# A graph network kernel on one core: one more group of columns copied by VectorE, and the hand-made jobs begun earlier

## The chip, the cores and the metric

The kernel runs on one core of one Trainium2 chip. The metric is the device time in microseconds. The engines are named as in the profile: PE is TensorE (PEld its weight loads), DVE is VectorE, ACT is ScalarE, POOL is GpSimd and SP is SyncE, which here only issues DMAs.

## The reference, cut to what matters

```python
h = relu(layernorm(x))                              # x: 12500 nodes x 128
m = relu(concat(h[src], h[dst], edge_attr) @ w1 + b1) @ w2 + b2   # 400000 edges, sorted by dst
agg = segment_sum(m, dst)
out = x + gru(agg, h)                               # gates r, z, n over w_ih, w_hh
```

The edges are sorted by their target node `dst`; their source nodes `src` are random. So a row per edge has to be fetched by `src`, 400,000 in all.

## The kernel before, in words

**Ahead of the loop.** The first stage normalises all nodes, keeps h transposed on the chip (`hT_all`, 128 features x 12500 nodes) and stores the table A = h @ w1[0:128] in HBM, so that an edge needs one row of A instead of a matmul. It also stores B, the part of the target nodes.

**Groups and units.** The edges form 3125 tiles of 128. Eight tiles make a group, 391 groups in all (the first has five tiles); a group is worked in two units of four tiles, units 0 to 781. Units -7 to -1 run ahead of the loop and hold only the steps that work ahead. In unit u the function `stages` (L1151) issues: the statistics of raw rows for unit u+7 (`raw_stats`, VectorE, and a root on ScalarE, L234), their end and the norms for u+6 (`raw_fin`, and `raw_h`, four norms on ScalarE, L292), the turning of the raw rows for u+4 (`raw_turn`: TensorE L699, copied by VectorE L701), the matmuls of u+3 (`pre`, L716), the one-hot tables (L615, L666), and the add of the fetched rows for u+2 (`add`, VectorE, once for a whole group in its second unit; L748). Behind it `seg` (L774) sums the edges of unit u into their nodes. Every engine takes its instructions in this order.

**Where the rows of a group come from.** Four ways:

- Groups 0 to 8 (`RAW`) are fetched by GpSimd from x, since A is not there yet; they need statistics, norms, turning and a relu on ScalarE (L760).
- Most groups are fetched by GpSimd from A, one indirect DMA for a tile (`gather`, L158, issued at L170). The fetched rows lie in 11 buffers G that go round (`GBUFS`, `ring`, L149). So a gather for the group at place j of this ring waits until the group at place j-11 has let go of its buffer: a raw group at its turning, another at its add.
- 30 groups go to VectorE and 29 to ScalarE as **column jobs**: a gather of 1024 columns of `hT_all` on the chip, four bytes on each partition at a time, by an address in a register. ScalarE copies them one by one (`one_by_one`, L1062, register loads of 16 at L1049); VectorE takes two columns in one instruction (`Pairs`, L1021, register loads of 32), and untangles 64 pairs by a byte copy (L1032). TensorE then multiplies with w1 (L727), and the add becomes a plain relu on VectorE (L743).
- 5 groups go to SyncE as **row jobs**: 1024 row DMAs from A.

**Who gets which group, and when.** `SPREAD` (L57) has the counts and `START` (L58) the unit at which each engine's first job begins. The loop at L92 spreads the groups evenly between START//2+2 and a fixed distance from the end. A job runs from the end of the one before (or START) to a few units before its group is needed: 2k-4 for ScalarE, 2k-6 for VectorE, 2k-8 for SyncE. ScalarE's and SyncE's jobs are cut into four phases of a unit (`run_jobs`, L1118): phase 0 ahead of `stages`, the others behind it. VectorE's pairs go by the due numbers of `pairs_due` (L1069), put around long instructions by `before_long`, `some` and `behind_long`. Before the change ScalarE's first groups are 17, 30, 43 and VectorE's 21, 34, 46; the last are 388 and 386.

**The places.** The source numbers of the groups in jobs are brought as rows of a table `at` (`at_row`, L448, DMAs on SyncE's queue in the first stage). One VectorE instruction (L1209) scales them to addresses (`place_of` holds factor and offset for each row). Row 64 of `at` is used by another step, so that a 65th job gets row 65 (`row_of`), and two small fills make row 64 whole.

Of the kernel before, what the change touches and what calls it, by code (L numbers as in the profile page):

```python
# [17 lines left out]
ALU = mybir.AluOpType  # L18
# [35 lines left out]
STEP = {"act": 4, "sp": 4}  # L54
QUEUE = 10
ROW = 4 * D
SPREAD = {"dve": 30, "act": 29, "sp": 5}  # L57
START = {"dve": 14, "act": 4, "sp": 24}  # L58
NR = 12672

H_AT = 16512
# [3 lines left out]
def tile_gnn(ctx: ExitStack, tc: tile.TileContext, x, src, srcT, dstT, dstP, eaT, eaP, w1, b1, w2T, b2,  # L65
             wih, bih, whh, bhh, out):
    nc = tc.nc
# [23 lines left out]

    mode, order = {}, {m: [] for m in SPREAD}  # L92
    for m, n in SPREAD.items():
        lo, hi = START[m] // 2 + 2, NP - {"dve": 5, "act": 3, "sp": 12}[m]
        for i in range(n):
# [34 lines left out]
    at = const.tile([128, PAIR * 128], I32, name="at")  # L130
# [71 lines left out]
    def row_of(k):  # L202
        r = by_hand.index(k)
        return r if r < 64 else r + 1

    ROWS = row_of(by_hand[-1]) + 1
# [3 lines left out]
    place_of = const.tile([ROWS, 2], F32, name="place_of")  # L210
# [397 lines left out]
    def onehot_T(k):  # L608
        if k >= NP:
            return  # L610
        c = slice((k % QP) * 512, (k % QP + 1) * 512)
        o, i = Ls[k // QP][:2 * V, c], Ls[k // QP].bitcast(I32)[:2 * V, c]
        n = k - BLOCKS[-1][0]
        if n < 0:
            nc.vector.tensor_scalar(o, i, node_of[:, k:k + 1], None, op0=ALU.is_equal)  # L615
        else:
            nc.vector.tensor_scalar(o, i, node_of[:, k:k + 1], 0.0, op0=ALU.is_equal, op1=ALU.add,
                                    accum_out=dlast[:2 * V, n:n + 1])
# [58 lines left out]
    def raw_h(u):  # L677
        if u < 2 * RAW:
            for i, s in enumerate(slots(u)):
                relu_norm(unit(u)[:, s, :], unit(u)[:, s, :], HE[u][:, i, :])  # L680

    def raw_stats(u):
        if u < 2 * RAW:
            l = slots(u)
            HE[u] = bn_sqrt(p2, bn(p2, lambda j: unit(u)[:, l[j], :], 128, len(l)), 128, len(l))

    def raw_fin(u):
        if u < 2 * RAW:
            n = len(slots(u))
            st = p2.tile([128, GRP, 2], F32, name="st_raw", bufs=4)  # L690
            bn_fin(p2, st[:, :n, :], HE[u], 128, n)
            HE[u] = st

    def raw_turn(u):
        if u < 2 * RAW:
            l = slots(u)
            pt = ps1.tile([128, 512], F32, name="misc")
            for i, s in enumerate(l):
                nc.tensor.transpose(pt[:, i * 128:(i + 1) * 128], unit(u)[:, s, :], ident)  # L699
            hT = p3.tile([128, 512], F32, name="gt", bufs=3)  # L700
            nc.vector.tensor_copy(hT[:, :len(l) * 128], pt[:, :len(l) * 128])  # L701
            HE[u] = hT
# [54 lines left out]
    def relu(u):  # L757
        if u in RT:
            o, p = RT.pop(u)
            nc.scalar.activation(o, p, AF.Relu)  # L760
# [276 lines left out]
    def one_by_one(m, k):  # L1037
        et = {"act": ET.Activation, "sp": ET.SP}[m]
        r = row_of(k)
        if m == "sp":  # L1040
            goal[k] = tc.alloc_semaphore(f"brought{r}"), 16 * PAIR * 128
            G[k] = pj.tile([128, GRP, 2, D], F32, name="G_sp", bufs=1)
            rows = G[k].bitcast(U8)
        else:
            hand[k] = pj.tile([128, PAIR * 128], F32, name=f"HE_{m}")
            he = hand[k].bitcast(U8)
        for e0 in range(0, PAIR * 128, LOAD[m]):
            low, high = (0, ROW * (N - 1)) if m == "sp" else (H_AT, H_AT + 4 * (N - 1))
            _, vals = nc.values_load_multi_w_load_instructions(  # L1049
                at[r:r + 1, e0:e0 + LOAD[m]], engines=[et], min_val=low, max_val=high,  # L1050
                skip_runtime_bounds_check_because="src holds numbers of nodes")
            for i, v in enumerate(vals):
                e = e0 + i
                if m == "sp":
                    a, j = divmod(e // 128, GRP)
                    fetched = put(rows[e % 128:e % 128 + 1, j, a, :],
                                                A_bytes[bass.ds(v, ROW)].rearrange("(o f) -> o f", o=1))
                    fetched.then_inc(goal[k][0], 16)
                    tc.no_tile_sem_insts.add(fetched.ins.name)
                    tc.add_to_no_dep_group(f"rows{k}", fetched.ins)  # L1060
                else:
                    nc.scalar.copy(he[:, e * 4:e * 4 + 4], column(v))  # L1062
                if i % STEP[m] == STEP[m] - 1:
                    yield
# [4 lines left out]
    def pairs_due():  # L1069
        start, n = START["dve"], 0  # L1070
        for k in order["dve"]:
            end = 2 * k - 6
            for u in range(start, end):
                due[u] = n + -(-(PAIR * 64 * (u + 1 - start)) // (end - start))
            n += PAIR * 64
            start = end
# [3 lines left out]
    def behind(u):  # L1080
        return due.get(u, cols.end if u >= START["dve"] else 0) - cols.done

# [4 lines left out]
    def before_long(u, ops):  # L1087
        if u == START["dve"]:
            cols.load()
        some(u, cols.end, QUEUE - ops)  # L1090
        if cols.turn and u % 2 == 0:
            some(u, cols.end, QUEUE - ops - 1)
            cols.part()

    def behind_long(u, least):
        if behind(u) >= least:
            cols.pairs(cols.left())
            cols.load()
# [9 lines left out]
    for m in ("act", "sp"):  # L1108
        start = START[m]
        for k in order[m]:  # L1110
# [5 lines left out]
    PH = 4  # L1116

    def run_jobs(u, phase):  # L1118
        if phase == 0:
            for m, k, span in jobs.get(u, ()):  # L1120
                live[m] = [one_by_one(m, k), u, span, PAIR * 128 // STEP[m], 0]
        for m, job in list(live.items()):
            it, start, span, steps, done = job
            want = -(-steps * ((u - start) * PH + phase + 1) // (span * PH))
            while job[4] < want:
                job[4] += 1
                if next(it, "end") == "end":
                    del live[m]
                    break
# [4 lines left out]
    def gathers(u):  # L1134
        while asked[0] < NP and (asked[0] in mode or 2 * taker[asked[0]] + 1 < u + 2):
            gather(asked[0])
            asked[0] += 1
# [13 lines left out]
    def stages(u):  # L1151
        if u + 7 >= 0:
            raw_stats(u + 7)
        if u + 6 >= 0:
            raw_fin(u + 6)
            raw_h(u + 6)
        if u + 4 >= 0:
            raw_turn(u + 4)
        if u + 3 >= 0:
            pre(u + 3)  # L1160
        before_long(u, 2 if u % 4 == 2 else 1)
        if u % 2 == 0:
            onehot_T(u // 2 + 3)
            onehot(u // 2 + 3)
        if u + 2 >= 0:
            add(u + 2)
            relu(u + 2)
        behind_long(u, 1)

    for u in range(-7, 0):  # L1170
        stages(u)
    nodes_left = []

    def step(left):
# [13 lines left out]
    for u in range(NU):  # L1188
        k, h = divmod(u, 2)
        gathers(u)  # L1190
        if h == 0:
            window_rows(k + 4)
            if k % QP == 1:
                fetch(k // QP + 3)
            if k and k == BLOCKS[block(k)][0]:
                nodes_left.append([node(block(k) - 1), 2 if k < BLOCKS[-1][0] else 1])
            if k % PLACE == 1:
                indices(k // PLACE + 2)
            if k % PLACE == 5:
                place(k // PLACE + 1)  # L1200
                dst_tile(k // PLACE + 2)
            if k == 6:
                late_setup()
            if k == 20:
                store_stats()
            if k == NP - 20:
                check_windows()
        if u == min(START.values()) - 2:
            nc.vector.tensor_scalar(at[:ROWS, :], at[:ROWS, :], place_of[:, 0:1], place_of[:, 1:2],  # L1209
                                    op0=ALU.mult, op1=ALU.add)  # L1210

        run_jobs(u, 0)
        stages(u)
        run_jobs(u, 1)
        some(u, 4, QUEUE - 1)
        run_jobs(u, 2)
        some(u, 4, QUEUE - 1)
        seg(u)
        if u == 0:
            node_setup()  # L1220
        run_jobs(u, 3)
        some(u, cols.end, QUEUE - 1)
        worked[0] = False
        if h == 0:
            take(k - 1)
        step(nodes_left)
        if u in LAST_STEPS:
            next(last)
        behind_long(u, 4 if worked[0] else 14)
        in_time(u)  # L1230
# [173 lines left out]
```

## Time and profile before

| what | before |
|---|---|
| median of 3 runs | 3344.64 us (3341.72 to 3346.97) |
| the profiled execution | 3339.77 us, span 3338.0 us |
| TensorE's mean granted clock in it | 0.807 |
| gathers of GpSimd (L170) | 69 from x, 2544 from A |
| column copies of ScalarE (L1062) | 29696 |
| column pairs of VectorE (L1021) | 15360 |
| row DMAs of SyncE into G_sp | 5120 |

How to read it: the span is from the first to the last instruction, and the 1.8 us beside it lie around them. A row of a group shows the line, the engine, the operation, output and input, the count; then busy time and the mean duration of one in ns; then the engine's idle time just ahead of these instructions and what ended most of it. "issue" stands for idle time in which nothing that the profile shows was waited for. A row of the timeline shows the start in us, the duration in us, the instruction, and in brackets the idle time ahead of it with what ended it. A duration includes the pipeline's ends, so instructions of one engine overlap a little; the pitch of a series is taken from start to start.

### The profile page before, as it was taken

To read this page: it belongs to the slowest core of one execution; us is meant where nothing else is said; L and a number is where in the kernel's file an instruction comes from. 1 tells how busy PE (TensorE), PEld (TensorE's weight loads), DVE (VectorE), ACT (ScalarE), POOL (GpSimd) and SP (SyncE) were. 2 spreads that over 40 slices of the span, in tenths; PEclk is the share of its full clock that TensorE was granted. 3 is DMA by queue.
4 is the path that set the end of the run, shared out by engine and by line. 5 is a ranking of instruction groups with operands and counts; after the bars stand their busy time and mean duration, and the time that the engine had idled before them with its cause. 6 is when DMAs were issued, how large, how long until landed. Compare 5 with 4: busy or idle time off the path is not lost. (4 is left out here: it accounts for less than half of the span.)

```text
span 3338.0 us, 96341 instructions
## 1 busy us (share of the span) xinstructions
PE 2404.0 (72%) x13177; PEld 1556.9 (47%) x13177; DVE 2391.7 (72%) x17889; ACT 3133.3 (94%) x30026; POOL 2515.3 (75%) x2622
## 2 busy tenths in 40 slices
PE   7567777777777777767776777676677677767767
PEld 6444444444454445444444444454344444444445
DVE  8567777777777777777767777776676777676765
ACT  6599999999999999999999989998989999899985
POOL 7777777777777777777777777777777777777775
PEclk9878878888877787878777878778787788777878
DMA  6433443444344444444343444443443444444332
GB/s 213 107 88 89 99 101 98 100 95 106 96 101 94 102 95 99 104 102 97 95 100 98 99 99 100 98 100 89 98 99 93 101 95 99 95 97 99 93 95 72
DMA packets 195740, 333.85 MB, mean 100 GB/s; under 512 B 68936, under 2 KB 117639, under 8 KB 195095
## 3 DMA queue, kind: packets, MB, share of 16 engines
q0 software_dynamic: 83616, 171.41, 22.6%
q1 hardware_dynamic: 111335, 156.20, 17.3%
q14 instruction: 536, 4.39, 0.4%
q8 instruction: 109, 1.79, 0.2%
q10 hardware_dynamic: 144, 0.07, 0.0%
HBM read 307.17 MB, written 20.24 MB: 98 GB/s over the span
## 5 line engine op out<-in xcount | busy, mean ns | idle before, releaser
L1062 ACT COPY HE_act<-hT_all 128x4 uint8 x29696 | 2990.7, 189 | 52.5 <-issue 27.5
L170 POOL DMA_INDIRECT G<-A,src_i x2544 | 2448.5, 962 | 782.4 <-issue 748.0
L1021 DVE SCALAR_TENSOR_TENSOR both<-hT_all 128x4 uint16 x15360 | 1314.9, 153 | 673.3 <-issue 635.7
L716 PE MATMUL pre<-RW,L 128*128 128x256 f32 x3128 | 1113.4, 481 | 10.4 <-DMA RW<-B 10.4
L774 PE MATMUL seg<-RB,OH 128*32 128x129 f32 x6250 | 610.5, 327 | 668.7 <-DVE RB L748 577.4
L774 PEld LDWEIGHTS seg<-RB,OH 128*32 128x32 f32 x6250 | 335.2, 126 | 981.3 <-DVE RB L748 659.4
L716 PEld LDWEIGHTS pre<-RW,L 128*128 128x128 f32 x3128 | 653.5, 233 | 286.5 <-issue 212.9
L748 DVE CUSTOM_DVE_ANT_0 RB<-pre,G 128x1024 f32<-128x1024 f32 x319 | 386.0, 1210 | 83.8 <-DMA G<-A,src_i 76.6
L615 DVE TENSOR_SCALAR L<-L,node_of 64x512 f32<-64x512 int32 x382 | 188.5, 493 | 51.8 <-DMA L<-in_dstP 51.6
L666 DVE TENSOR_TENSOR OH<-dloc,seg 128x512 f32<-128x512 f16 (+1 forms) x198 | 131.1, 663 | 0.0
L801 PE MATMUL nd<-spot,sums 128*128 128x40 f32 x782 | 119.7, 325 | 9.4 <-DVE sums L783 9.4
L801 PEld LDWEIGHTS nd<-spot,sums 128*128 128x128 f32 x782 | 114.8, 235 | 18.7 <-DVE sums L783 10.2
L1032 DVE COPY HE_dve<-both 128x512 uint8<-128x512 uint8 x240 | 103.4, 431 | 0.0
L727 PEld LDWEIGHTS pre<-w1a,HE_act 128*128 128x128 f32 x464 | 87.4, 234 | 12.6 <-ACT HE_act L1062 1.8
L806 PE MATMUL misc<-spot_h,dcol 128*128 128x40 f16 x382 | 45.3, 194 | 66.5 <-DVE dcol L831 61.4
L727 PEld LDWEIGHTS pre<-w1a,HE_dve 128*128 128x128 f32 x480 | 84.8, 221 | 9.5
L727 PE MATMUL pre<-w1a,HE_act 128*128 128x128 f32 x464 | 85.9, 316 | 1.4 <-ACT HE_act L1062 1.4
L727 PE MATMUL pre<-w1a,HE_dve 128*128 128x128 f32 x480 | 83.8, 304 | 0.0
L170 POOL DMA_INDIRECT G<-in_x,src_i x69 | 65.4, 947 | 21.8 <-issue 20.7
L851 PE MATMUL nd<-DEG,brow 34*128 34x512 f32 (+2 forms) x112 | 65.6, 667 | 20.5 <-ACT gt L861 18.7
L743 DVE TENSOR_SCALAR RB<-pre 128x1024 f32<-128x1024 f32 x59 | 71.6, 1213 | 7.0 <-PE pre L727 6.9
L806 PEld LDWEIGHTS <-dcol 128*128 128x128 f16 x382 | 37.0, 105 | 81.0 <-DVE dcol L831 69.8
(178 smaller groups left out, 1357.0 us busy)
## 6 DMA issues: line engine op xcount, KB each, us to landing
G_sp<-A SPq DMA_DIRECT2D x5120, 0.5 KB
L<-in_dstP SPq DMA_DIRECT2D x195, 256.0 KB
L<-in_eaP SPq DMA_DIRECT2D x195, 256.0 KB
G<-A,src_i POOLq DMA_INDIRECT x2544, 3.3
RW<-B SPq DMA_DIRECT2D x782, 16.0 KB
xb<-in_x SPq DMA_DIRECT2D x26, 256.0 KB
out<-xb SPq DMA_DIRECT2D x26, 256.0 KB
xs<-in_x SPq DMA_DIRECT2D x11, 512.0 KB
```

The lines of the kernel that those rows point to most:

```text
L170: fetched = nc.gpsimd.indirect_dma_start(out=G[k][:, j, a, :], out_offset=None, in_=table, in_offset=bass.IndirectOffsetOnAxis(ap=src_i[c] ...
L615: nc.vector.tensor_scalar(o, i, node_of[:, k:k + 1], None, op0=ALU.is_equal)
L666: nc.vector.tensor_tensor(p, dloc[:, e0:e1, None].to_broadcast(shape), row[:, None, :].to_broadcast(shape), op=ALU.is_equal)
L716: nc.tensor.matmul(p[:, 2 * i:2 * i + 2, :], Ls[k // QP][:, c0:c0 + 128], RW[k % 4], start=True, stop=not raw)
L727: nc.tensor.matmul(p[:, 2 * i + a, :], cols, w1a, start=False, stop=n + 1 == len(l) or l[n + 1][1] != j)
L748: made = nc.vector._custom_dve(TENSOR_ADD_SAT, out=o, in0=p, in1=G[k].rearrange("p j a f -> p (j a) f")[:, c, :], s0=float("inf"), s1=0.0)
L774: nc.tensor.matmul(p[r0:r0 + V, :D + 1], OH[k][:, a * GRP + j, :], RB[k % 2][:, 2 * j + a, :D + 1], start=False, stop=all(b != a for _, _, ...
L801: nc.tensor.matmul(p[:, bass.ds(offs[i], V + SHIFT)], sums[:, slot(b, i), :D], spot[:, i % 2, :], start=False, stop=i == len(offs) - 1)
L806: nc.tensor.matmul(p[:, bass.ds(offs[i], V + SHIFT)], t[:, c:c + 128], spot_h[:, a, :], start=False, stop=i == len(offs) - 1)
L1021: nc.vector.scalar_tensor_tensor(self.both[:, e % PIECE // 2, :], column(second), 256.0, column(first), op0=ALU.mult, op1=ALU.add)
L1032: nc.vector.tensor_copy(hand[k].bitcast(U8)[:, p0 * 4:(p0 + PIECE) * 4].rearrange("p (n c b) -> p n c b", c=2, b=4), both.bitcast(U8).rear ...
L1062: nc.scalar.copy(he[:, e * 4:e * 4 + 4], column(v))
```

## The change

VectorE gets 31 groups instead of 30. The first jobs begin at unit 8 for VectorE (14 before), -6 for ScalarE (4 before) and 8 for SyncE (24 before), and the groups are spread anew from these starts: ScalarE's first groups are now 12, 25, 39, VectorE's 18, 30, 42; the last are 388 and 386 as before. The scaling of the places moves from unit 2 of the loop to a place ahead of unit -7, and the units ahead of the loop call `run_jobs` as the loop does. With 65 jobs the table `at` has 66 rows. The groups that GpSimd fetches go from 327 to 326.

```diff
-SPREAD = {"dve": 30, "act": 29, "sp": 5}
-START = {"dve": 14, "act": 4, "sp": 24}
+SPREAD = {"dve": 31, "act": 29, "sp": 5}
+START = {"dve": 8, "act": -6, "sp": 8}
...
+    nc.vector.tensor_scalar(at[:ROWS, :], at[:ROWS, :], place_of[:, 0:1], place_of[:, 1:2],
+                            op0=ALU.mult, op1=ALU.add)
     for u in range(-7, 0):
+        run_jobs(u, 0)
         stages(u)
+        for phase in range(1, PH):
+            run_jobs(u, phase)
...
-        if u == min(START.values()) - 2:
-            nc.vector.tensor_scalar(at[:ROWS, :], at[:ROWS, :], place_of[:, 0:1], place_of[:, 1:2],
-                                    op0=ALU.mult, op1=ALU.add)
-
         run_jobs(u, 0)
         stages(u)
```

## The prediction

> **What bounds the kernel now.** I read the page's first and fifth parts, then GpSimd's waits and its timeline.
>
> ```profile
> PE 2404.0 (72%) x13177; PEld 1556.9 (47%) x13177; DVE 2391.7 (72%) x17889; ACT 3133.3 (94%) x30026; POOL 2515.3 (75%) x2622
> L1062 ACT COPY HE_act<-hT_all 128x4 uint8 x29696 | 2990.7, 189 | 52.5 <-issue 27.5
> L170 POOL DMA_INDIRECT G<-A,src_i x2544 | 2448.5, 962 | 782.4 <-issue 748.0
> L1021 DVE SCALAR_TENSOR_TENSOR both<-hT_all 128x4 uint16 x15360 | 1314.9, 153 | 673.3 <-issue 635.7
> ```
>
> By busy share ScalarE (94%) looks like the bound and GpSimd (75%) does not. But GpSimd's 782.4 us of idle time are nearly all "issue": a fixed gap ahead of each gather. The waits of GpSimd, and four rows of its timeline:
>
> ```profile
> POOL G L170 <- issue: 768.8, 2521, 0.3
> POOL G L170 <- DVE RB L748: 5.9, 14, 1.9
> ```
> ```profile
> 124.75 0.94 POOL L170 DMA_INDIRECT G<-A,src_i  x1 [2.49 <-PE misc L699]
> 206.81 0.94 POOL L170 DMA_INDIRECT G<-A,src_i  x1 [1.91 <-DVE RB L748]
> 237.26 0.95 POOL L170 DMA_INDIRECT G<-A,src_i  x1 [0.30 <-issue]
> 3319.33 0.94 POOL L170 DMA_INDIRECT G<-A,src_i  x1 [0.30 <-DMA G<-A,src_i]
> ```
>
> A gather takes (2448.5+782.4)/2544 = 1.270 us from start to start, and they run back to back until 3320.3 us; the span ends at 3338. Nothing holds GpSimd after 206.81 us: there it waited 1.9 us for the add of group 9 (L748), which frees the buffer that group 22 needs. From then on GpSimd alone sets the end. Who reads its rows is behind it at first and catches up late:
>
> ```profile
> DVE both L1021 <- issue: 311.0, 394, 2.6
> DVE RB L748 <- DMA G<-A,src_i: 76.6, 31, 5.8
> ```
>
> This is VectorE's waiting from 1800 us to the end: 31 adds waited for rows, 76.6 us. So two things move the end: the number of gathers, one for one, and anything that delays GpSimd's restart at 206.81, also one for one, since that wait was already above the fixed gap.
>
> **What goes: eight gathers.** VectorE takes a 31st group, so 8 x 1.270 = 10.2 us leave GpSimd. The jobs that end last stay on groups 386 (VectorE) and 388 (ScalarE), so the 17.7 us behind the last gather stay. 10.2 is thus the most that this part can give.
>
> Against it stand eight more byte copies of VectorE (L1032). Two gathers beside such a copy:
>
> ```profile
> 242.67 0.41 DVE L1032 COPY HE_dve<-both 128x512 uint8<-128x512 uint8 x1
> 251.00 0.42 DVE L1032 COPY HE_dve<-both 128x512 uint8<-128x512 uint8 x1
> ```
> ```profile
> 242.26 0.95 POOL L170 DMA_INDIRECT G<-A,src_i  x1 [0.30 <-issue]
> 251.00 1.24 POOL L170 DMA_INDIRECT G<-A,src_i  x1 [0.30 <-issue]
> ```
>
> The copy that begins 0.4 us into a gather leaves it at 0.95; the one that begins with it lengthens it to 1.24. Bounds: 0 to 8 x 0.30 = 2.4 us. I take 0, since most gathers stand at 0.94 and the mean of 0.962 holds all lengthening there is. The Trainium skill (SBUF — State Buffer, section Who interferes with whom) says that a VectorE copy in a two-port mode and a GpSimd instruction lock each other out for a whole instruction, whichever issues first. By that rule eight copies of 0.42 would give back at most 3.4 us; the pair of rows agrees with its order of issue, not with a full block.
>
> **What moves: ScalarE's first job.** It used to begin in unit 4 and ends up in unit -6. Its 1024 copies go over 26 units either way (30-4, now 20+6), 39.4 a unit; ten units of them, 396 with the rounding to steps of four, come ahead of unit 4. Where ScalarE stands there now:
>
> ```profile
> 90.00:143.00 53.00, 25.63 (x151) 20.44 (x152) 29.73 (x168) 20.88 (x53) 36.73 (x39) 0.71 0.39 101
> 143.00:206.00 63.00, 39.95 (x271) 31.75 (x271) 34.81 (x203) 62.96 (x493) 46.97 (x50) 0.89 0.34 84
> ```
>
> From 90 to 143 it is busy 20.9 of 53 us; from 143 to 206 it is busy throughout (62.96 of 63). So an idle stretch of 32.1 us is offered 396 copies, and behind it no room is left. The copies' pitch and that of the work between, from ScalarE's timeline:
>
> ```profile
> 103.22 0.30 ACT L234 ACTIVATE s<-mv,eps 128x4 f32<-128x4 f32 x1 [10.58 <-DVE mv L229]
> 104.24 0.88 ACT L292 ACTIVATE G<-G,st_raw 128x128 f32<-128x128 f32 x2 [0.73 <-DVE st_raw L247]
> 124.77 0.30 ACT L234 ACTIVATE s<-mv,eps 128x4 f32<-128x4 f32 x1 [10.88 <-DVE mv L229]
> 142.95 1.23 ACT L1062 COPY HE_act<-hT_all 128x4 uint8 x12
> 145.82 4.04 ACT L1062 COPY HE_act<-hT_all 128x4 uint8 x40
> 149.76 0.29 ACT L234 ACTIVATE s<-mv,eps 128x4 f32<-128x4 f32 x1
> 149.96 1.63 ACT L292 ACTIVATE G<-G,st_raw 128x128 f32<-128x128 f32 x4
> 151.50 1.00 ACT L760 ACTIVATE RB<-pre 128x1024 f32<-128x1024 f32 x1
> 152.41 4.06 ACT L1062 COPY HE_act<-hT_all 128x4 uint8 x40
> ```
>
> Start to start, 40 copies take 3.94 us (98.5 ns each), a root 0.20, four norms 1.54, a relu 0.91. In program order 52 copies (unit -6 and the first phase of -5) stand ahead of the root at 103.22, which waits for VectorE, and fit into its 10.58 us; 5 us of that wait stay idle. The two norms at 104.24 end by 105.1. From there to unit 4: 344 copies x 0.0985 = 33.9, eight roots 1.6, eight times four norms 12.3, three relus 2.7, in all 50.5 us, so unit 4 begins at 155.6 instead of 142.95: **12.7 us late**. With the copies at the mean of their whole group, (2990.7+52.5)/29696 = 102.5 ns, it is 14.1. The later roots find their statistics ready: the one that waited until 124.77 is now reached at about 126 (105.1, 156 copies, three roots, twelve norms). I take 13.
>
> Is this lateness passed on? From 143 on ScalarE has no gap, and the order of its work in units 4 to 13 is what it was. The relu of group 6 lets TensorE turn the last raw rows, for which VectorE waits:
>
> ```profile
> 187.63 1.00 ACT L760 ACTIVATE RB<-pre 128x1024 f32<-128x1024 f32 x1
> ```
> ```profile
> 101.29 0.48 DVE L615 TENSOR_SCALAR L<-L,node_of 64x512 f32<-64x512 int32 x1 [9.95 <-DMA L<-in_dstP]
> 190.84 0.69 DVE L701 COPY gt<-misc 128x512 f32<-128x512 f32 x1 [3.45 <-PE misc L699]
> 193.39 0.73 DVE L1021 SCALAR_TENSOR_TENSOR both<-hT_all 128x4 uint16 x8 [1.85 <-issue]
> 205.33 1.21 DVE L748 CUSTOM_DVE_ANT_0 RB<-pre,G 128x1024 f32<-128x1024 f32 x1
> 239.66 1.21 DVE L748 CUSTOM_DVE_ANT_0 RB<-pre,G 128x1024 f32<-128x1024 f32 x1
> ```
>
> The chain is relu at 187.63, copy at 190.84 (3.45 us waited), VectorE's queue in order, the add of group 9 at 205.33, GpSimd at 206.81. No link has slack.
>
> **VectorE's column jobs** now begin in unit 8, not 14, at 512 pairs over 22 units (23.3 a unit) in both. A pair costs 1314.9/15360 = 86 ns, with the idle time behind register loads (1314.9+635.7)/15360 = 127 ns. In units 8 to 12 they mostly fill waits for ScalarE. In unit 13, behind the copy at 190.84, one unit of pairs is new: 2.0 to 3.0 us, less up to 1.85 us of first load that is over earlier. If VectorE falls behind already in units 8 to 12, I allow 2 us more. Bounds 0 to 5; I take 2.
>
> **A second wait of GpSimd.** With group 12 taken by ScalarE, the buffer needed three groups after group 22 is that of group 13, not 12. GpSimd was at 237.26 then; the add of group 13 ended at 239.66+1.21 = 240.9. Both shift alike, so GpSimd waits 3.6 us plus the 0.3 from an add's end to a gather: 3.9, bounds 3.6 to 4.7.
>
> **Taken at nothing.** The scaling (L1209), the row loads from HBM (L107) and ScalarE's register loads (L1049):
>
> ```profile
> L1209 DVE TENSOR_SCALAR at<-at,place_of x1: 876/876/876, 134.1 to 134.1; 64x1024 int32<-64x1024 int32 x1
> L107 SPq DMA_DIRECT2D at<-in_src x64: 238/254/839, 21.4 to 83.7; - x64
> L1049 ACTq TENSOR_LOAD <-at x1856: 1007/1045/2193, 140.6 to 3301.6; - x186
> ```
>
> The scaling moves from 134.1 to about 88, ahead of VectorE's 9.95 us wait at 101.29, which hides it; without that cover, 0.9. The 65th row is one more issue of 0.25 us on SyncE by 84, before the scaling; two small fills are paid early by VectorE, at most 0.5. SyncE's five jobs start 16 units sooner at the same rate, about seven row loads a unit (7 x 0.25 = 1.8 us of a 4 us unit): 0, at most 3 if they delay a load of L that VectorE then waits for.
>
> **Sum.** -10.2 + 13 + 2 + 3.9 = **+8.7 us**. Against the profiled execution (3339.77, span 3338.0) that is 3348.5; the median of the three runs is 4.9 higher, so I predict 3344.6 + 8.7 = **3353.3**. Its own bounds: 12.7 to 14.1, 0 to 5, 3.6 to 4.7, and 0 to 3 and 0 to 2.4 for the rest give +6.1 to +19, with most of it from +6 to +14.
>
> **Rivals.**
>
> Copies hidden by their loads (faster). Each 16 copies need a register load of 1.045 us in ScalarE's queue, while 16 copies take 1.576 at the pitch above. If the load is the price and runs on behind norms and waits, a copy costs (1.576-1.045)/16 = 33 ns, 344 of them 11.4 instead of 33.9, and unit 4 is not late at all. Then GpSimd restarts at 206.8 to 209 and waits again for 0 to 3.9: -10.2 to -4, 3334 to 3341. Against it: the 40 copies at 145.82 follow four norms directly and show no hidden load. It decides from the first copies ahead of the loop: a pitch under 60 ns.
>
> VectorE becomes the bound (slower still). 512 more pairs at 127 ns are 65 us; some 140 pairs are drawn ahead of the add of group 9, so 373 fall behind it, 47 us, against a spare of 76.6-10.2 = 66. At the mean duration and all idle time, 153 + 673.3/15360 = 197 ns a pair, it would be 73, and the reader ends 7 us after the rows: +16, 3361. For it speaks that both sides are of one size; against it, that 153 ns is a duration and not a pitch. It decides if the adds never wait for rows at the end.
>
> The early jobs do not start early. If the first load waits for hT_all or the places until 103 or later, the 52 copies lose their cover, 5 us more delay: +14, 3358. If they were held back as far as unit 4, the loop would begin on time and only the gathers and the second wait change: -6, 3338. The last row load is issued at 83.7, 4 us before the scaling's new place, which speaks against both.
>
> **Chances.** The forecast's mechanism 0.70, of which 0.17 small enough to lie within 0.2% (+6.7); copies hidden 0.15; VectorE as bound 0.10; not early 0.05. What a measurement of this kernel can tell from no change is about 0.2%, 6.7 us. With 0.13 of the hidden copies and 0.02 of the last case counted as faster, and 0.02 of the hidden copies as no change: faster 0.15, same 0.20, slower 0.65. The range 3341 to 3364 leaves out most of the hidden copies (0.13) and the far ends (0.05).
>
> **What would show it.** In the changed profile: 2605 gathers; ScalarE's copies from about 90 us; its first copy that belonged to unit 4 near 156; GpSimd held long before the first gather of group 22, near 222 instead of 206.81, and again three groups later by some 4 us; no hold after 350; the last gather near 3328, with the adds still waiting for rows after 2200 us. It is wrong if GpSimd passes 207 on time, or if its last gather has long been done when the reader arrives.

## The result, and the profile after

| what | before | after |
|---|---|---|
| median of 4 runs each | 3343.44 us (3341.72 to 3346.97) | 3362.49 us (3360.74 to 3364.20) |
| the profiled execution | 3339.77, span 3338.0 | 3360.74, span 3358.9 |
| gathers, first to last | 69 + 2544 | 69 + 2536 |

The change makes the kernel **slower**: the ratio is 1.0056, 95% interval 1.0038 to 1.0073, that is 12.7 to 24.4 us with 19 in the middle. Between the two profiled executions the spans differ by 20.9 us. The profiled execution is the fastest of its kernel each time, that of before by more (3.7 us below the median of 3343.44, that of after 1.7 below 3362.49), so that the spans differ by some 2 us more than the medians. The forecast was +8.7, its range reached to +19.4. The sign and the place are as forecast, the size is about twice it.

The first and fifth parts of the page of after. The columns are those of before.

```profile
PE 2379.5 (71%) x13193; PEld 1542.5 (46%) x13193; DVE 2430.6 (72%) x18411; ACT 3133.4 (93%) x30026; POOL 2513.5 (75%) x2614
L170 POOL DMA_INDIRECT G<-A,src_i x2536 | 2446.6, 965 | 805.4 <-issue 744.7
L1062 ACT COPY HE_act<-hT_all 128x4 uint8 x29696 | 2991.4, 189 | 55.9 <-issue 28.1
L1021 DVE SCALAR_TENSOR_TENSOR both<-hT_all 128x4 uint16 x15872 | 1355.0, 153 | 698.8 <-issue 663.9
```

The busy shares have hardly moved; from the page alone one could not say why the kernel is slower. The line to look at is GpSimd's: eight gathers less, and yet 23 us more of idle time ahead of them (805.4 against 782.4), 3.3 us less of it "issue". What ended the rest stands in GpSimd's waits (us in total, times, the longest), and its place in GpSimd's timeline:

```profile
POOL G L170 <- DVE RB L748: 20.5, 15, 12.0
POOL G L170 <- PE misc L699: 14.9, 6, 3.5
```
```profile
227.87 0.94 POOL L170 DMA_INDIRECT G<-A,src_i  x1 [12.05 <-DVE RB L748]
262.32 0.94 POOL L170 DMA_INDIRECT G<-A,src_i  x1 [4.50 <-DVE RB L748]
3340.62 0.94 POOL L170 DMA_INDIRECT G<-A,src_i  x1 [0.30 <-DMA G<-A,src_i]
```

GpSimd waits 20.5 us for adds instead of 5.9, 16.6 of them in two places: ahead of group 22 it is held until 227.87 instead of 206.81, and three groups of its ring later, until 262.32, where it had passed at 237.26 without a wait. Behind that no wait is longer than 0.6 us, up to the last gather, which ends at 3341.56. The second row, waits for TensorE, stands ahead of both: five of the six lie between 156.40 and 206.12, where GpSimd needs the buffers of raw groups, whose turning ScalarE's lateness now delays. They lie within the first stretch below, and do not add to it: group 22 goes when the add of group 9 is done, however early GpSimd stands there. From these rows and those of before the whole difference can be added up:

| stretch | before | after | more |
|---|---|---|---|
| start to the first gather of group 22 | 206.81 | 227.87 | +21.1 |
| from there to the second hold's end | 30.45 | 34.45 | +4.0 |
| from there to the end of the last gather | 3083.0, 2432 gathers of 1.2677 | 3079.2, 2424 of 1.2703 | -3.8 |
| behind it to the end of the span | 17.7 | 17.3 | -0.4 |
| span | 3338.0 | 3358.9 | +20.9 |

The third row is -10.1 for eight gathers and +6.4 for a pitch that is 2.6 ns longer over 2424 of them.

**Why group 22 is late.** ScalarE's timeline of after, and the row of before in which unit 4's root stands:

```profile
92.56 1.24 ACT L1062 COPY HE_act<-hT_all 128x4 uint8 x12 [1.10 <-DVE st_raw L245]
104.22 0.30 ACT L234 ACTIVATE s<-mv,eps 128x4 f32<-128x4 f32 x1 [5.13 <-DVE mv L229]
105.89 4.05 ACT L1062 COPY HE_act<-hT_all 128x4 uint8 x40
109.84 0.29 ACT L234 ACTIVATE s<-mv,eps 128x4 f32<-128x4 f32 x1
156.91 0.29 ACT L234 ACTIVATE s<-mv,eps 128x4 f32<-128x4 f32 x1
200.65 1.00 ACT L760 ACTIVATE RB<-pre 128x1024 f32<-128x1024 f32 x1
```
```profile
144.08 0.30 ACT L234 ACTIVATE s<-mv,eps 128x4 f32<-128x4 f32 x1
```

The copies begin at 92.56; 40 of them take 3.95 us (105.89 to 109.84), 98.7 ns each, the same pitch as in the loop. Unit 4's root comes 12.8 us late (156.91 against 144.08), and the relu of group 6 13.0 us late (200.65 against 187.63). The windows of before showed ScalarE 20.9 us busy from 90 to 143; after (us of PE, PEld, DVE, ACT and POOL in order):

```profile
90.00:143.00 53.00, 21.32 (x119) 16.77 (x120) 27.95 (x156) 45.28 (x348) 37.43 (x40) 0.70 0.40 105
```

It is 24.4 us more busy, and 7.7 us stay idle. Most of this is one wait, 5.1 us for VectorE ahead of the root at 104.22: only 52 copies stand before that root in ScalarE's order, and the next must wait behind it. VectorE adds to this. Its copies of the turned raw rows (L701) are one to a unit, so they can be laid side by side. First those of before, with the waits for ScalarE between them, then those of after:

```profile
162.86 0.68 DVE L701 COPY gt<-misc 128x512 f32<-128x512 f32 x1
168.63 0.18 DVE L240 RECIPROCAL y<-s 128x4 f32<-128x4 f32 x1 [3.44 <-ACT s L234]
169.57 0.68 DVE L701 COPY gt<-misc 128x512 f32<-128x512 f32 x1
174.23 0.18 DVE L240 RECIPROCAL y<-s 128x4 f32<-128x4 f32 x1 [1.83 <-ACT s L234]
175.16 0.68 DVE L701 COPY gt<-misc 128x512 f32<-128x512 f32 x1
180.81 0.18 DVE L240 RECIPROCAL y<-s 128x4 f32<-128x4 f32 x1 [3.97 <-ACT s L234]
181.78 0.68 DVE L701 COPY gt<-misc 128x512 f32<-128x512 f32 x1
186.12 0.68 DVE L701 COPY gt<-misc 128x512 f32<-128x512 f32 x1
```
```profile
176.29 0.68 DVE L701 COPY gt<-misc 128x512 f32<-128x512 f32 x1
184.23 0.68 DVE L701 COPY gt<-misc 128x512 f32<-128x512 f32 x1
190.02 0.68 DVE L701 COPY gt<-misc 128x512 f32<-128x512 f32 x1
195.24 0.18 DVE L240 RECIPROCAL y<-s 128x4 f32<-128x4 f32 x1 [1.40 <-ACT G L292]
196.18 0.68 DVE L701 COPY gt<-misc 128x512 f32<-128x512 f32 x1
203.49 0.68 DVE L701 COPY gt<-misc 128x512 f32<-128x512 f32 x1
208.55 0.69 DVE L701 COPY gt<-misc 128x512 f32<-128x512 f32 x1 [1.24 <-issue]
226.38 1.22 DVE L748 CUSTOM_DVE_ANT_0 RB<-pre,G 128x1024 f32<-128x1024 f32 x1
```

Subtract each row of before from its partner (the waits are those for ScalarE and TensorE; idle time behind register loads, "issue", is not counted as one):

| from copy to copy | pairs before, after | VectorE's wait there before | took before, after | lateness at its end |
|---|---|---|---|---|
| (at 162.86 / 176.29) | | | | 13.4 |
| to 169.57 / 184.23 | 0, 23 | 3.44 | 6.71, 7.94 | 14.7 |
| to 175.16 / 190.02 | 0, 16 | 1.83 | 5.59, 5.79 | 14.9 |
| to 181.78 / 196.18 | 0, 25 | 3.97 | 6.62, 6.16 | 14.4 |
| to 186.12 / 203.49 | 0, 23 | none | 4.34, 7.31 | 17.4 |
| to 190.84 / 208.55 | 0, 25 | 3.45 | 4.72, 5.06 | 17.7 |
| to the add of group 9, 205.33 / 226.38 | 71, 103 | none | 14.49, 17.83 | 21.05 |

ScalarE's 13 us are there before the first early pair is drawn. Where VectorE used to wait, the pairs cost 1.2, 0.2, -0.5 and 0.3 us; in the two stretches without a wait they cost 3.0 and 3.3. Together 7.6 us. Behind 195.24 VectorE no longer waits for ScalarE at all on the way to the add of group 9. This split goes by the order of time; it does not say what each early start would cost without the other.

### The profile page after: what moved, and what is told of

It is laid out like the page before. It is cut to its first block, busy times and chain, and to the rows that moved or that the text cites. A ratio compares the mean times of both kernels' runs of the same rounds, so it can differ in the third digit from the quotient of the medians.

```text
span 3358.9 us, 96915 instructions
## 1 busy us (share of the span) xinstructions
PE 2379.5 (71%) x13193; PEld 1542.5 (46%) x13193; DVE 2430.6 (72%) x18411; ACT 3133.4 (93%) x30026; POOL 2513.5 (75%) x2614
## 3 DMA queue, kind: packets, MB, share of 16 engines
q1 hardware_dynamic: 111337, 156.20, 17.3%
## 5 line engine op out<-in xcount | busy, mean ns | idle before, releaser
L170 POOL DMA_INDIRECT G<-A,src_i x2536 | 2446.6, 965 | 805.4 <-issue 744.7
L1021 DVE SCALAR_TENSOR_TENSOR both<-hT_all 128x4 uint16 x15872 | 1355.0, 153 | 698.8 <-issue 663.9
L748 DVE CUSTOM_DVE_ANT_0 RB<-pre,G 128x1024 f32<-128x1024 f32 x318 | 384.7, 1210 | 74.7 <-DMA G<-A,src_i 73.4
L615 DVE TENSOR_SCALAR L<-L,node_of 64x512 f32<-64x512 int32 x382 | 185.6, 486 | 13.6 <-DMA L<-in_dstP 13.6
L666 DVE TENSOR_TENSOR OH<-dloc,seg 128x512 f32<-128x512 f16 (+1 forms) x198 | 131.1, 662 | 0.0
L801 PE MATMUL nd<-spot,sums 128*128 128x40 f32 x782 | 104.2, 299 | 13.8 <-DVE sums L783 13.8
L801 PEld LDWEIGHTS nd<-spot,sums 128*128 128x128 f32 x782 | 99.3, 207 | 22.0 <-DVE sums L783 14.6
L1032 DVE COPY HE_dve<-both 128x512 uint8<-128x512 uint8 x248 | 108.0, 436 | 0.2 <-issue 0.2
L727 PEld LDWEIGHTS pre<-w1a,HE_act 128*128 128x128 f32 x464 | 80.5, 217 | 9.1
L170 POOL DMA_INDIRECT G<-in_x,src_i x69 | 65.5, 950 | 21.9 <-issue 20.7
L743 DVE TENSOR_SCALAR RB<-pre 128x1024 f32<-128x1024 f32 x60 | 72.8, 1214 | 5.2 <-PE pre L727 5.2
```

The lines of the kernel that those rows point to most:

```text
L170: fetched = nc.gpsimd.indirect_dma_start(out=G[k][:, j, a, :], out_offset=None, in_=table, in_offset=bass.IndirectOffsetOnAxis(ap=src_i[c] ...
L666: nc.vector.tensor_tensor(p, dloc[:, e0:e1, None].to_broadcast(shape), row[:, None, :].to_broadcast(shape), op=ALU.is_equal)
L727: nc.tensor.matmul(p[:, 2 * i + a, :], cols, w1a, start=False, stop=n + 1 == len(l) or l[n + 1][1] != j)
L748: made = nc.vector._custom_dve(TENSOR_ADD_SAT, out=o, in0=p, in1=G[k].rearrange("p j a f -> p (j a) f")[:, c, :], s0=float("inf"), s1=0.0)
L801: nc.tensor.matmul(p[:, bass.ds(offs[i], V + SHIFT)], sums[:, slot(b, i), :D], spot[:, i % 2, :], start=False, stop=i == len(offs) - 1)
L1021: nc.vector.scalar_tensor_tensor(self.both[:, e % PIECE // 2, :], column(second), 256.0, column(first), op0=ALU.mult, op1=ALU.add)
```

## The experiments

**My theory.** GpSimd's gate is the release of buffers by the adds of groups 9 and 13. ScalarE's early copies move it by 13 us, VectorE's early pairs by some more, and the eight gathers cannot pay for it. **Rivals:** VectorE as the bound of the whole loop (31 groups too many); SyncE's early row loads in the way of other loads; or something that 31 groups cost apart from when they begin. I undid parts of the change (START and SPREAD), and moved the gate by a twelfth buffer.

### One part at a time

Four kernels, each made from the changed one by its two lines SPREAD and START, in this order: 31 groups with the old starts, ScalarE early alone, VectorE early alone, all but ScalarE early.

```diff
-SPREAD = {"dve": 31, "act": 29, "sp": 5}
-START = {"dve": 8, "act": -6, "sp": 8}
...
+SPREAD = {"dve": 31, "act": 29, "sp": 5}
+START = {"dve": 14, "act": 4, "sp": 24}
...
+SPREAD = {"dve": 30, "act": 29, "sp": 5}
+START = {"dve": 14, "act": -6, "sp": 24}
...
+SPREAD = {"dve": 30, "act": 29, "sp": 5}
+START = {"dve": 8, "act": 4, "sp": 24}
...
+SPREAD = {"dve": 31, "act": 29, "sp": 5}
+START = {"dve": 8, "act": 4, "sp": 8}
```

> The 31st VectorE group alone, all jobs starting as before the change (units 14, 4 and 24). Gate theory: only eight gathers go and GpSimd restarts at 206 to 209 us on the buffer of group 9, so the time falls by about 10 us (3334, ratio 0.997). Load theory (the extra group makes VectorE the reader that ends last, or slows the gathers themselves): no gain or a loss, 3343 to 3352; the gathers' pitch would be 1.270 us or more instead of 1.268.

> ScalarE's start at unit -6 alone: 30 VectorE groups, VectorE from unit 14, SyncE from 24. Gate theory: the relu of group 6 comes 13 us late, VectorE's path behind it is as before, so GpSimd restarts 13 us late (near 220) and waits again 4 us for group 13's buffer: +17, 3360. Rival (the lateness is VectorE's own, of its early pairs): restart below 212 and a time within 5 us of the kernel before.

> VectorE's start at unit 8 alone: 30 groups, ScalarE from unit 4, SyncE from 24. Gate theory with the measured term: the pairs of units 8 to 13 make the add of group 9 later by the 8 us that VectorE added in the changed kernel, restart near 215, no second wait, +8: 3351. If ScalarE's lateness is needed for VectorE to fall behind, the add is within 3 us of before: 3343 to 3346.

> The change with ScalarE's part undone: 31 groups, VectorE and SyncE from unit 8, ScalarE from unit 4. Gate theory: -10 for the gathers, +8 for VectorE's early pairs, restart near 215, no second wait: -2, 3341. If ScalarE's early start were harmless it would stay at 3362.

This first set ran on a chip on which the kernel before itself takes 5874 us, so all four were run a second time; that set ran on another chip, and there the kernel before takes 5869 us. The chips with some 3345 us are called the usual ones below.

> The 31st VectorE group alone (starts 14, 4 and 24), again, on a chip where the kernel before takes about 3345 us. Gate theory: restart on group 9's buffer at 205 to 209 us, eight gathers fewer: ratio 0.997, -10 us, give or take 5 for the gathers' pitch, which has stood between 1.268 and 1.274 us in the runs so far. Load theory: no gain or a loss.

> ScalarE's start at unit -6 alone, again. Gate theory: restart 13 us late (218 to 221), a second hold of some 4 us three groups later, +17: ratio 1.005. If VectorE's early pairs are what makes the restart late: restart below 212, ratio under 1.002.

> VectorE's start at unit 8 alone, again. Gate theory with the measured term: restart near 215, no second hold, +8: ratio 1.0024. If VectorE falls behind only together with ScalarE: restart below 210, ratio 1.000 to 1.001.

> The change with ScalarE's part undone (31 groups, VectorE and SyncE from unit 8, ScalarE from unit 4), again. Gate theory: -10 for the gathers, +8 for the restart: ratio 0.999 to 1.000, 20 us below the changed kernel. If ScalarE's early start is harmless: ratio 1.005.

| kernel | ratio to the kernel before on its chip, first set | second set |
|---|---|---|
| 31 groups, old starts | 0.9973 (0.9958 to 0.9988) | 0.9967 (0.9954 to 0.9979) |
| ScalarE early alone | 0.9988 (0.9978 to 0.9997) | 0.9972 (0.9960 to 0.9984) |
| VectorE early alone | 1.0023 (1.0013 to 1.0034) | 1.0031 (1.0019 to 1.0044) |
| all but ScalarE early | 1.0016 (1.0007 to 1.0026) | 1.0021 (1.0009 to 1.0033) |

Before these ratios are held against the expectations, one must ask whether the same thing bounds the kernel there. Two rows of the waits in the kernel with 31 groups and the old starts (second set):

```profile
POOL G L170 <- DVE RB L748: 2352.2, 214, 42.8
ACT HE_act L1062 <- issue: 2235.3, 3059, 1.9
```

It does not. GpSimd waits 2352 us for adds, up to 42.8 at a time, where it waited 5.9 on the usual chip, and ScalarE's copies wait 2235 us for "issue" where it was 27.5. So on these two chips GpSimd is held by those who use its rows, all through the kernel, and the gathers do not set the end; a late gate need not cost anything there. What in the expectations rests on a gate that sets the end is neither borne out nor refuted by these ratios. That two of them come out as expected (0.997 for 31 groups, 1.0024 for VectorE early) is thus no support, and two do not: all but ScalarE early was expected at 0.999 to 1.000, and ScalarE early alone, the main cost in my account, at 1.005, where it comes out 0.1 to 0.3% faster. Why these chips are so was not looked into.

The first 350 us can still be used, since the kernels of a set ran on one chip, and the first of them has the old starts. The relu of group 6 (ScalarE) and the first gather of group 22 (GpSimd), for 31 groups with old starts, then ScalarE early alone, then VectorE early alone, all of the second set:

```profile
297.87 1.00 ACT L760 ACTIVATE RB<-pre 128x1024 f32<-128x1024 f32 x1
321.75 0.94 POOL L170 DMA_INDIRECT G<-A,src_i  x1 [10.25 <-DVE RB L748]
```
```profile
324.49 1.00 ACT L760 ACTIVATE RB<-pre 128x1024 f32<-128x1024 f32 x1
346.95 0.95 POOL L170 DMA_INDIRECT G<-A,src_i  x1 [8.46 <-DVE RB L748]
```
```profile
300.94 1.00 ACT L760 ACTIVATE RB<-pre 128x1024 f32<-128x1024 f32 x1
326.54 0.95 POOL L170 DMA_INDIRECT G<-A,src_i  x1 [11.67 <-DVE RB L748]
```

ScalarE's early start by itself moves its relu by 26.6 us and group 22 by 25.2; VectorE's early start by itself moves group 22 by 4.8, and all but ScalarE early by 8.6 (330.32). The first set gives 25.8, 3.6 and 7.2. On the usual chip the whole change gave 13.0 (the relu) and 21.1 (group 22). The sizes differ, since ScalarE's copies come with those waits for "issue" between them, but the order is the one of my account: each of the two starts delays the gate by itself, and ScalarE's carries most of it. A second hold shows too. The gather three groups behind group 22 with ScalarE early alone, second set:

```profile
400.84 0.95 POOL L170 DMA_INDIRECT G<-A,src_i  x1 [19.11 <-DVE RB L748]
```

In the first set it is held 18.3 us; in the six other runs, where group 12 stays in the ring, it is held at most 0.5. This is weak support, since those six have holds of 10 to 13 us one group away. What each start alone costs the whole kernel on a usual chip was not tried.

### A twelfth buffer

With 12 buffers a gather waits for an add one place further back. The room comes from a small temporary of the first stage that is laid into another tile.

```diff
-GBUFS = 11
+GBUFS = 12
-        off_c = pool.tile([128, NB * 16], F32, name="off_c", bufs=1)[:1, :].rearrange("o (b n) -> o b n", n=16)
+        off_c = OHB[2][0:1, :, :].rearrange("o t v -> o (t v)")[:, :NB * 16].rearrange("o (b n) -> o b n", n=16)
```

In the changed kernel:

> The changed kernel with 12 buffers for fetched rows instead of 11 (a temporary of the first stage lies in an unused table to make room). Gate theory: GpSimd gets one more group done before it needs group 9's buffer, so it is held about 10 us less: -10 against the changed kernel, 3352. If GpSimd's late restart were not what sets the end, the time stays at 3362.

In the kernel before:

> The kernel before with 12 buffers. Gate theory: it loses only the two short holds (2.2 us at 124.75 and 1.6 us at 206.81): -4, 3340. If buffers mattered beyond the gate it would gain more than 8.

These ran on a chip on which the kernel before takes 3348.36 us, 4.9 more than in the first comparison. The changed kernel with 12 buffers gave 3359.80, ratio 1.0039 (1.0025 to 1.0053), against 1.0056 (1.0038 to 1.0073) with 11: 5.7 us less in the middle, give or take some 7.5 (the two half-widths added in squares), which leaves room for the expected 10 as well as for none. Its GpSimd timeline:

```profile
207.30 0.94 POOL L170 DMA_INDIRECT G<-A,src_i  x1 [4.30 <-PE misc L699]
229.07 0.94 POOL L170 DMA_INDIRECT G<-A,src_i  x1 [12.08 <-DVE RB L748]
263.30 0.94 POOL L170 DMA_INDIRECT G<-A,src_i  x1 [4.27 <-DVE RB L748]
3341.00 0.95 POOL L170 DMA_INDIRECT G<-A,src_i  x1 [0.31 <-issue]
```

The gate moves as the theory wants it: group 22 starts at 207.30, the two holds are as long as before (12.08 and 4.27) and end some 1 us later, but now in front of groups 23 and 27. So eight gathers more are over at 263, about 9 us ahead (8 x 1.25, the distance of two gathers in the timeline, less the 1.0 by which the second hold ends later). Yet the last gather begins at 3341.00, no earlier than in after. Over the 2416 gathers behind the hold the pitch is 1.2743 us where it was 1.2703: 2416 x 0.0040 = 9.7 us, all of it given back in this profiled execution. But the two profiles belong to two comparisons, and the kernel before was not profiled in the second one; how much of the longer pitch comes with its 4.9 us is open. The hold is confirmed by the trace; that an earlier gate shortens the kernel is not, by time: inconclusive.

The kernel before with 12 buffers gave 0.9994 (0.9985 to 1.0003), no difference. Its hold at group 22 is gone:

```profile
203.55 0.94 POOL L170 DMA_INDIRECT G<-A,src_i  x1 [0.30 <-issue]
```

3.3 us earlier than 206.81, at a pitch that again was longer (1.2723 against 1.2677). A gain of 4 us would be a ratio of 0.9988; the interval holds it, and holds none at all as well.

### SyncE early alone

```diff
-SPREAD = {"dve": 31, "act": 29, "sp": 5}
-START = {"dve": 8, "act": -6, "sp": 8}
+SPREAD = {"dve": 30, "act": 29, "sp": 5}
+START = {"dve": 14, "act": 4, "sp": 8}
```

> SyncE's start at unit 8 alone, all else as before the change. Gate theory: nothing on GpSimd's path, within 2 us of the kernel before (3343). Rival (the early row jobs delay transfers or slow the gathers): +3 to +6, with a gathers' pitch above 1.268 us.

Measured: 0.9996 (0.9987 to 1.0005). Group 22 starts on time:

```profile
205.47 0.94 POOL L170 DMA_INDIRECT G<-A,src_i  x1 [0.73 <-DVE RB L748]
```

By time SyncE's start has no part in the loss: the interval ends at +0.05%, 1.7 us, and the rival wanted 3 to 6. The rival's other sign, a pitch above 1.268, is there: 1.2702, as long as in the changed kernel. The kernel before was not profiled in this comparison, so whether SyncE's start lengthens the pitch is not shown.

### More groups off GpSimd without early starts

```diff
-SPREAD = {"dve": 31, "act": 29, "sp": 5}
-START = {"dve": 8, "act": -6, "sp": 8}
+SPREAD = {"dve": 31, "act": 29, "sp": 6}
+START = {"dve": 14, "act": 4, "sp": 8}
```

> A version aimed at being faster: 31 VectorE groups, six row jobs of SyncE from unit 8 instead of five from 24, VectorE from unit 14 and ScalarE from unit 4 as before. Gate theory: sixteen gathers fewer and the restart on time: -20, 3323. Rival (the reader side is full): VectorE or SyncE ends after the rows, the adds stop waiting for rows, gain under 10.

A miss: 3635.02 us, ratio 1.0866 (1.0851 to 1.0881). It should have taken away 16 gathers at no cost. The waits of VectorE and GpSimd:

```profile
DVE L L615 <- DMA L<-in_dstP: 302.1, 105, 10.1
POOL G L170 <- DVE RB L748: 242.2, 63, 16.4
```

VectorE's wait of the same kind in the kernel before:

```profile
DVE L L615 <- DMA L<-in_dstP: 51.6, 22, 9.9
```

And SyncE's queue in the run with six jobs (start and duration of a series, in us):

```profile
394.94 5.84 SPq L107 DMA_DIRECT2D G_sp<-A  x16
400.95 0.82 SPq L107 DMA_DIRECT2D RW<-B  x2
401.88 8.64 SPq L107 DMA_DIRECT2D G_sp<-A  x20
```

In these two series a row DMA with its address from a register takes 5.84/16 = 0.37 and 8.64/20 = 0.43 us of SyncE, not the 0.25 that I had read from the loads of `at`. Six jobs need 6144 of them, so at these prices some 2250 to 2650 us of SyncE's queue (an estimate), with the loads of L, RW and the rest behind them in order. VectorE waits 302 us for L (51.6 before), the adds come late, and GpSimd waits 242 us for them. By these waits the bound has gone from GpSimd to SyncE's queue. With five jobs from the same unit 8 the kernel lost nothing (above), which points at the sixth. So the sixth job is no way out, and the kernel with 31 groups and nothing else, worth 10 us by my account, is measured only where the gathers do not bind (0.997). No version here is shown to beat the kernel before where they do.

## Why the prediction was right, and where its size failed

- **What bounds the kernel: right.** GpSimd has no wait above 0.6 us behind 262.32, and the spans differ by what happened ahead of it (+25.1) and by the gathers behind it (-3.8). This is read from the two traces; no run shows by time that the hold alone lengthens the kernel, since the twelfth buffer left that open. The rival in which VectorE becomes the bound falls. VectorE's waits of after, from 1700 us to the end:

```profile
DVE RB L748 <- DMA G<-A,src_i: 73.4, 31, 6.1
```

  31 adds still wait for rows, 73.4 us; before it was 76.6 us, 31 times, in the same part of the kernel. The 512 pairs more are found again in VectorE's busy and idle time (1355.0+663.9 against 1314.9+635.7 for the pairs, 68 us), but not at the end.
- **Eight gathers, -10.2: right** (-10.1 by the pitch of before). The eight byte copies at nothing: the pitch is 2.6 ns longer, +6.4 us, above the 2.4 that I allowed for the eight. It cannot be theirs alone: gathers of more than 1.0 us went from 230 to 241, but the kernel before with 12 buffers, which has no extra copy, has 275. What made the pitch longer stays open; see the last section.
- **ScalarE 13 us late: right**, 12.8 at unit 4's root and 13.0 at the relu. The copies kept their full pitch, 98.7 ns, so the rival of hidden copies falls, and they began at 92.56, so the last rival falls too. The link that passed the lateness on is not the one of the prediction, though. There it was the relu of group 6, behind which VectorE's copy stood 3.2 us (187.63 to 190.84, with a wait for TensorE). After the change that copy comes 7.9 us behind the relu (200.65 to 208.55) and its wait is "issue". ScalarE's lateness had entered VectorE's queue earlier, through the roots and norms, the last time at 195.24 (14.4 us behind its partner at 180.81); from there on VectorE's own work sets the time.

- **A second wait of 3.9: right**, 4.5 less the 0.3 of an ordinary gap is 4.2, and the stretch grew by 4.0.
- **VectorE's early pairs, +2 in bounds of 0 to 5: this is the step that failed.** They cost 7.6 to 8 us (21.06 of delay, 13.0 of it ScalarE's). The prediction put it: "In units 8 to 12 they mostly fill waits for ScalarE." By the table above that holds for four of five units, where the pairs cost 1.2, 0.2, -0.5 and 0.3. It fails for the stretch from 181.78 to 186.12, in which VectorE clears and fills tables (L557 to L567) and had no wait: 23 pairs there cost 3.0 us. And the last stretch, for which I had 2.0 to 3.0, less up to 1.85, cost 3.3: 32 pairs more, not 23, and a byte copy of 0.42, with nothing taken off. I had looked at VectorE's waits as a sum and not at whether each unit has one.
- **SyncE at nothing: right**, by the run of its own (0.9987 to 1.0005), although a row load costs 0.37 to 0.43 and not 0.25 us; its part in the pitch stays open.
- **What is left.** 7.6 instead of 2 is 5.6, and 6.4 of pitch is the rest: 8.7 + 5.6 + 6.4 = 20.7, against 20.9 in the spans. The first is in the schedule and shown by the trace; the cause of the second is not shown, and it may differ from one execution to the next. That the time still lies inside the range is partly luck: these two terms lie outside their own bounds (7.6 against 5; 6.4 against the 2.4 allowed for slower gathers), and the others stayed inside theirs.

## What to carry to other kernels

An engine with idle time ahead of the loop is not free room if its queue must be through by a given time: count what the idle stretch holds (here 32 us, of which 24 came to be used) against what is put into it (396 copies of 0.0985 us, 39 us), and follow the overflow to whoever waits for it. When work is to vanish in another engine's waits, lay the units side by side one by one: a unit without a wait pays in full, whatever the waits add up to. And before a run is held against a theory, see in its trace that the same engine still sets the end there.

## What the runs showed of the hardware

**A gather's duration goes with what VectorE does when it begins.** I sorted all gathers from A by the VectorE instruction that runs when they begin, in five profiles from usual chips (before, after, SyncE early, and 12 buffers before and after). Those that begin beside the comparison of L615 (64x512, 0.49 us) last 1.09 to 1.12 us on average, those beside the byte copy L1032 1.07 to 1.08, those beside the adds, the plain relu or L666 0.94, and 0.94 where no VectorE instruction runs. One such pair, of the changed kernel with 12 buffers:

```profile
1004.74 0.48 DVE L615 TENSOR_SCALAR L<-L,node_of 64x512 f32<-64x512 int32 x1
1004.86 1.17 POOL L170 DMA_INDIRECT G<-A,src_i  x1 [0.31 <-issue]
```

The Trainium skill (SBUF — State Buffer, Who interferes with whom) names `copy`, `cast` and `tensor_scalar` as operations that can take the port pair shared with GpSimd in a two-port mode, and says that the other side then blocks fully. The trace agrees for L615 and L1032; the plain relu L743, a TENSOR_SCALAR too but on `pre` in PSUM, lengthens nothing (0.94). In this pair the gather is 0.23 longer than 0.94, where L615 still had 0.36 us to run (1005.22 less 1004.86), so that less than the whole rest of it is added. How many gathers are lengthened differs between the profiles: 230 lasted over 1.0 us in the kernel before, 241 in the changed one, 267 with SyncE early, 275 and 302 with 12 buffers (before and changed). With them goes the mean duration:

```profile
L170 POOL DMA_INDIRECT G<-A,src_i x2544 | 2454.1, 965 | 781.3 <-issue 751.5 <-DVE both L1021 7.9 <-DVE RB L748 3.8
```
```profile
L170 POOL DMA_INDIRECT G<-A,src_i x2536 | 2456.1, 968 | 795.9 <-issue 748.8 <-DVE RB L748 18.8 <-DVE both L1021 7.3
```

These are SyncE early and the changed kernel with 12 buffers; the pitch behind the start went from 1.2677 (before) over 1.2702 and 1.2703 to 1.2723 and 1.2743. Over some 2430 gathers the ends of that range are 16 us apart, as much as most edits here were to bring. The last two, and SyncE early, come from the comparison in which the kernel before takes 4.9 us more; if all of that were pitch, it would be 2.0 ns (an estimate, 4.9 us over 2432 gathers). Whether gathers and such instructions meet by chance or by the schedule was not tried.

**The same program can take 5870 us.** On two of the chips ScalarE stands idle for "issue" ahead of its copies, 2235 us in the second set and 2228 in the first (31 groups, old starts), against 27.5 in the kernel before on a usual chip. TensorE's mean granted clock is 0.67 there, where it is 0.80 to 0.81 in the other profiles with some 3345 us. The runs do not show why.
